# Building a graph's adjacency matrix on TensorE: edges by fixed chunks with sized windows, or by groups of ten targets

## The chip, the cores and the metric

The kernel runs on one core of a Trainium2 chip. The metric is the device time of one execution in microseconds; runs of the same kernel are compared by their median. Within a core, TensorE (PE) multiplies, VectorE (DVE) and ScalarE (ACT) do elementwise work, GpSimd (POOL) fills constants, and SyncE (SP) issues most of the transfers. Each engine works through its own instructions in order; semaphores tie them together.

## The reference

A graph has 1250 nodes with 512 features and 20,000 edges `src -> dst`, with the edges **sorted by dst**. Two graph layers follow each other, with a layer norm before and a residual after each. Cut to what matters here:

```
h  = relu(layernorm(x))
# layer 0
xn   = batchnorm(h)
agg  = segment_sum(xn[src], dst) / max(deg, 1)
conv = relu(agg @ W_conv + b_conv)
attn = kernel attention over the first 256 nodes (h @ Wq, h @ Wk, h @ Wv, random features, @ Wo)
x    = x + batchnorm(conv + attn + h)
# layer 1
h  = relu(layernorm(x))
z  = (1 + eps) * h + segment_sum(h[src], dst)
x  = x + h + relu(batchnorm(relu(batchnorm(z @ W1 + b1)) @ W2 + b2))
```

Both segment sums use the same edges. The kernel therefore builds a dense adjacency matrix of counts once (`adj`: 1250 sources in ten tiles of 128 rows, by 1250 targets), and both sums become products with it.

## The kernel before

**Two stages matter here.** `tile_gnn` (L1416) loads the edges and prepares keys: this is the prologue. It then loads the number `bad` into a register of every engine and branches: `sorted_graph` if the edges fit the plan, `any_graph`, a slow general arm, if they don't. At the start of `sorted_graph` the adjacency is built, with the attention's projections, the layer norms of the other nodes and the key features laid between its steps.

**How an adjacency is counted.** Take a set of edges, one edge in each of 125 partitions. Two one-hot matrices are made by VectorE with `is_equal` (`onehots`, L207): `op` marks the row of the source within its tile (128 columns), `ok` marks the pair of source tile and target within a window (10 tiles times the window's width). The matmul of `op` and `ok` then adds one for each edge in the right cell, in PSUM (`count`, L227). VectorE writes the one-hots of two chunks interleaved (the last index `i` of 2), which makes runs of 16-bit values.

**Fixed chunks, windows by position.** The 20,000 edges are 160 chunks of 125 in order. As the edges are sorted, chunk c has targets near a known place, and `width(c)` and `window(c)` (L54, L58) say at building time which targets it may touch: 24 wide at the ends, 38 in the middle. The prologue checks that each edge lies in its window. PSUM blocks hold 50 targets (`TB`), and a window that crosses a block's edge is cut by `pieces` (L63), so that 160 chunks make 266 matmuls of 10 to 380 columns. A batch is 8 chunks: 20 batches, one `op` of 1024 and one `ok` of 1920 to 3040 elements each. When a block has got its last chunk, ACT copies it to `adj` (L240). There are two `op`/`ok` buffers and two PSUM blocks.

**What lies between the batches.** `beside` (L319) is a generator: each `next(rest)` after a batch puts in one step of the attention. In order: `first_nodes` (L252: layer norm and transposes of the first 256 nodes, kept in `ed.x0`), five steps of `features` for the keys (L272, with Wk), eight pairs of scores and values (L294, L363, with Wv), then the queries (L272, with Wq, which takes Wk's place in SBUF when the keys are done), the batch norm's statistics (L351), the exponentials of the keys (L402). `node()` puts in the layer norm of one more tile of 128 nodes (L107 to L116, transposes L246). A list scheduler orders the instructions of an engine, except those marked `order(...)`, which keep the order of the code; the whole prologue is so marked.

**The prologue.** Two transfers bring `dst` and `src` as 80 partitions of two chunks each; two more bring the first 256 rows of x. VectorE subtracts the middle of the window, takes the largest distance (L1481) for `bad`, and splits the source into row and tile (L1492, L1494). PE transposes the keys (L1513), so that edges come to lie in partitions, and ACT writes them as `prow` and `kcol` (L1514). ACT also sums the first rows of x, and their squares, for the layer norm (L1503). PE runs multiplications of zeros (`keep_up`) to stay warm.

**The SP queue** after the branch: Wk, proj, eight tiles of x, Wv, eleven small vectors, W_conv; later Wq, eps, Wo.

After the build come the first products with W_conv (`product`, L442), the attention's second half, and the rest of both layers.

Of the kernel before, what the change touches and what calls it, by code (L numbers as in the profile page):

```python
# [14 lines left out]
I32 = mybir.dt.int32  # L15
AF = mybir.ActivationFunctionType
# [20 lines left out]
S = 128  # L37
# [3 lines left out]
CE = 125  # L41
CH = E // CE
NG2 = CH // 2


WIDTHS = [(4, 24), (12, 30), (20, 34), (NG2, 38)]
WMIN, WMAX = WIDTHS[0][1], WIDTHS[-1][1]
TB = 50
BQ = 4
# [3 lines left out]

def width(c):  # L54
    return next(w for m, w in WIDTHS if min(c // 2, NG2 - 1 - c // 2) < m)


def window(c):  # L58

    return min(max((CE * c + 62) // 16 - width(c) // 2, 0), N - WMIN)  # L60


def pieces(c):  # L63

    w, n = window(c), width(c)
    assert w + n <= N and (n == WMIN or 0 < w < N - n)
    return [(b, max(w - b * TB, 0), min(w + n - b * TB, TB), max(b * TB - w, 0))
            for b in range(w // TB, (w + n - 1) // TB + 1)]
# [12 lines left out]
def sorted_graph(ctx: ExitStack, tc: tile.TileContext, ed, x, n1g, n1b, n2g, n2b, wconv, bconv,  # L81
# [7 lines left out]
    ident, iota2, prow, kcol, epsc = ed.ident, ed.iota2, ed.prow, ed.kcol, ed.epsc  # L89
    order = tc.keep_in_program_order  # L90

    def weight(w, name, pool, tag):
        k, n = w.shape[0] // 128, w.shape[1]
        t = pool.tile([128, k, n], F32, name=name, tag=tag)
        nc.sync.dma_start(t, w.rearrange("(k p) n -> p k n", p=128))
        return t
# [77 lines left out]
    wkt = weight(wk, "k", ap2, "w")  # L174
# [5 lines left out]
    wvt = weight(wv, "v", ap2, "w")  # L180
# [23 lines left out]

    prow, kcol = (t.rearrange("p g k -> p (g k)").rearrange("p (b q i) -> p b q i", q=BQ, i=2) for t in (prow, kcol))

    def onehots(bt, parts=(BQ,)):  # L207
        w = NJ * width(2 * BQ * bt)
        o = (WMAX - w // NJ) // 2
        op = ohp.tile([CE, BQ, S, 2], F16, name="op")  # L210
        ok = ohp.tile([CE, BQ, NJ * WMAX, 2], F16, name="ok")
        q = 0
        for n in parts:
            qs = slice(q, q + n)
            for t, keys, c0, k in ((op, prow, 0, S), (ok, kcol, o, w)):
                i = nc.vector.tensor_tensor(t[:, qs, :k, :],  # L216
                                            iota2[:, c0:c0 + k, :].unsqueeze(1).to_broadcast([CE, n, k, 2]),
                                            keys[:, bt, qs].unsqueeze(2).to_broadcast([CE, n, k, 2]), ALU.is_equal)
                if len(parts) > 1:
                    order(i)  # L220
            q += n
        return op, ok

    acc = {}
    left = [sum(1 for c in range(CH) if any(b == t for t, _, _, _ in pieces(c))) for b in range(N // TB)]

    def count(bt, op, ok):  # L227
        for q in range(BQ):
            for i in range(2):
                c = (bt * BQ + q) * 2 + i  # L230
                okc = ok[:, q, :NJ * width(c), i].rearrange("p (j w) -> p j w", w=width(c))
                for b, lo, hi, w0 in pieces(c):
                    first = b not in acc
                    if first:
                        acc[b] = accp.tile([S, NJ, TB], F32, name="acc")
                    left[b] -= 1
                    nc.tensor.matmul(acc[b][:, :, lo:hi], op[:, q, :, i], okc[:, :, w0:w0 + hi - lo],  # L237
                                     start=first, stop=(left[b] == 0), skip_group_check=True)
                    if left[b] == 0:
                        nc.scalar.copy(adj[:, :, b * TB:(b + 1) * TB], acc.pop(b))  # L240
# [11 lines left out]
    def first_nodes():  # L252
        rs = tmp.tile([S, NT], F32, name="rs0")
        nb = tmp.tile([S, NT], F32, name="nb0")
        nc.scalar.activation(rs, ed.sq0, AF.Sqrt, bias=epsc, scale=1.0 / D)
        nc.vector.reciprocal(rs, rs)
        nc.vector.tensor_tensor(nb, ed.mean0, rs, ALU.mult)
        for j in range(NT):
            t = tmp.tile([S, D], F32, name="hn", tag="row")
            nc.scalar.activation(t, ed.x0[:, j, :], AF.Relu, bias=nb[:, j:j + 1], scale=rs[:, j:j + 1])  # L260
            transposed(j, t)
# [57 lines left out]
    def beside():  # L319
# [14 lines left out]
        keys = features(wkt, "k")  # L334
# [7 lines left out]
        wqt = weight(wq, "q", ap2, "w")  # L342
# [77 lines left out]
    nbt = CH // (2 * BQ)  # L420
    ahead = onehots(0, (1, 1, 2))
    next(rest)
    for bt in range(nbt):
        oh, ahead = ahead, onehots(bt + 1, (BQ,) if bt else (2, 2)) if bt + 1 < nbt else None
        count(bt, *oh)
        next(rest, None)
# [86 lines left out]
    wot = weight(wo, "o", ap2, "w")  # L513
# [451 lines left out]
def any_graph(ctx: ExitStack, tc: tile.TileContext, x, src, dst, n1g, n1b, n2g, n2b, wconv, bconv,  # L965
# [20 lines left out]
    def weight(w, name, pool, tag):  # L986
# [3 lines left out]
        return t  # L990

# [171 lines left out]
    def features(w, name):  # L1163
        wt = weight(w, name, ap1, "w")
# [50 lines left out]
    wt = weight(wv, "v", ap1, "w")  # L1215
# [54 lines left out]
    wt = weight(wo, "o", ap1, "w")  # L1270
# [34 lines left out]
    wct = weight(wconv, "wconv", cp, "wconv")  # L1305
# [110 lines left out]
def tile_gnn(ctx: ExitStack, tc: tile.TileContext, x, src, dst, *rest):  # L1416
# [6 lines left out]
    ed.iota2 = pre.tile([CE, NJ * WMAX, 2], F16, name="iota2")  # L1423
    ed.prow = pre.tile([CE, NG2, 2], F16, name="prow")
    ed.kcol = pre.tile([CE, NG2, 2], F16, name="kcol")
    ed.x0 = pre.tile([S, NT, D], F32, name="x0")
    ed.mean0 = pre.tile([S, NT], F32, name="mean0")
    ed.sq0 = pre.tile([S, NT], F32, name="sq0")
    ed.epsc = pre.tile([128, 1], F32, name="epsc")
    ed.zeros = pre.tile([128, 512], F16, name="zeros")  # L1430
    flag = pre.tile([1, 2], F32, name="flag")
    bad = pre.tile([1, 1], I32, name="bad")
    with tc.tile_pool(name="raw", bufs=1) as raw, tc.tile_pool(name="rawp", bufs=1, space=PSUM) as rawp:
        dt = raw.tile([NG2, 2, CE], I32, name="dt")
        nc.sync.dma_start(dt, dst.rearrange("(g k e) -> g k e", k=2, e=CE))
        sr = raw.tile([NG2, 2, CE], I32, name="sr")
        nc.sync.dma_start(sr, src.rearrange("(g k e) -> g k e", k=2, e=CE))
        for j in range(NT):
            nc.sync.dma_start(ed.x0[:, j, :], x[j * S:(j + 1) * S, :])

        win = raw.tile([NG2, 2], I32, name="win")
        order(nc.gpsimd.iota(win, pattern=[[CE, 2]], base=62, channel_multiplier=2 * CE))
        iota1 = raw.tile([CE, NJ * WMAX], F16, name="iota1")
        order(nc.gpsimd.iota(iota1, pattern=[[1, NJ * WMAX]], base=0, channel_multiplier=0,
                             allow_small_or_imprecise_dtypes=True))
        wide = raw.tile([NG2, 1], F32, name="wide")
        order(nc.gpsimd.memset(wide, float(WMAX)))
        for (m, w) in reversed(WIDTHS[:-1]):  # L1450
            for base, step in ((-m, 1), (NG2 - 1 - m, -1)):
                order(nc.gpsimd.affine_select(out=wide, in_=wide, pattern=[[0, 1]], compare_op=ALU.is_ge,
                                              fill=float(w), base=base, channel_multiplier=step))
        order(nc.gpsimd.memset(ed.ident, 0.0))
        make_identity(nc, ed.ident, nomemset=True)
        order(nc.vector.memset(ed.epsc, EPS))
# [51 lines left out]
        for n, (t, c, shift) in enumerate(((pf, ed.prow, zero), (rel, ed.kcol, lift))):  # L1508
            if n == 0:
                total(0, zero, AF.Identity, sum0)  # L1510
# [45 lines left out]
```

## Time and profile before

| what | us |
|---|---|
| median of 3 runs | 386.99 (386.86 to 387.9) |
| the profiled execution | 388.38 |
| its span in the profile | 386.5 |
| PE busy in the span | 371.8 (96%), 1801 matmuls |
| VectorE busy in the span | 252.7 (65%) |
| ACT busy in the span | 159.8 (41%) |
| counting matmuls (L237), busy | 33.7, 266 matmuls |
| one-hot compares (L216), busy | 46.0, 46 instructions |

The profile shows one execution. A group's line reads: source line, engine, operation, output and inputs by the program's names, shapes, count, then busy time and the mean of one in ns, then idle time of the engine before it. A matmul's duration includes the time it takes to run through the array, while the next has already started, so durations of neighbours overlap and their sum exceeds the time they take. "Chain" means the work that ended last, followed back from the end of a stretch, each step to what released it.

### The profile page before, as it was taken

What the parts mean: (1) busy time and instruction counts of PE and PEld (TensorE: products, weight loads), DVE (VectorE), ACT (ScalarE), POOL (GpSimd) and SP (SyncE); (2) the same over time, 40 slices, a digit from 0 to 9 for tenths busy, and PEclk for the clock granted to TensorE, in tenths of its full rate; (3) what the DMA queues carried; (4) which work ended last, traced back from release to release, by engine and by line L of the source; (5) the groups of instructions that cost most, each with busy time, mean ns of one, the idle gap of its engine ahead of it and who ended that gap; (6) DMA issues with size and microseconds to landing.
All of it is one profiled execution on the core that took longest, in us unless ns stands there. A gap on an engine that the chain in (4) does not pass through costs nothing.

```text
span 386.5 us, 4859 instructions
## 1 busy us (share of the span) xinstructions
PE 371.8 (96%) x1801; PEld 270.1 (70%) x1801; DVE 252.7 (65%) x566; ACT 159.8 (41%) x312; POOL 36.6 (9%) x58
## 2 busy tenths in 40 slices
PE   7899999999999999999999999999999999999972
PEld 3666556648556579999867888777777777777751
DVE  6997999887758823869688522154782688412783
ACT  6687634973566443011136702132553452121230
POOL 5000000000000000500000006740044000000000
PEclk9899999999999999999999999999999999999995
DMA  4933002000000067000000000060000000000045
GB/s 143 362 122 109 2 0 110 0 2 1 2 1 0 2 209 273 2 0 3 0 1 2 0 0 2 0 217 3 0 0 3 1 0 2 0 0 1 2 133 140
DMA packets 13296, 17.83 MB, mean 46 GB/s; under 512 B 1453, under 2 KB 6669, under 8 KB 13265
## 3 DMA queue, kind: packets, MB, share of 16 engines
q1 hardware_dynamic: 10704, 16.19, 12.8%
q10 hardware_dynamic: 2560, 1.25, 1.2%
q8 instruction: 16, 0.26, 0.3%
q14 instruction: 16, 0.12, 0.1%
HBM read 14.88 MB, written 2.56 MB: 45 GB/s over the span
## 4 chain that ended last, share of the span: by engine, by line
PE 89%; DVE 6%; ACT 2%; issue 1%; DMA 1%; DVEq 0%; ACTq 0%
PE mm L785 28%; PE mm L728 12%; PE mm L596 11%; PE hw L442 8%; PE acc L237 7%; PE mm L272 4%; PE sc L294 3%; PE mm L542 2%; PE mm L470 2%; PE mm L503 2%; PE mm L363 2%; PE mm L246 2%; DVE xs L915 1%; PE mm L722 1%; PE mm L493 1%; PE mm L442 1%
## 5 line engine op out<-in xcount | busy, mean ns | idle before, releaser
L800 ACT ACTIVATE kept<-mm,vT 128x313 f32<-128x313 f32 x36 | 18.5, 520 | 49.6 <-PE mm L785 48.5
L237 PE MATMUL acc<-ok,op 125*128 125x380 f16 (+28 forms) x266 | 33.7, 271 | 0.0
L442 PE MATMUL hw<-wconv,xn 128*128 128x512 f32 (+1 forms) x72 | 33.4, 604 | 0.0
L728 PE MATMUL mm<-hi,adj 128*128 128x512 f32 (+2 forms) x100 | 32.1, 398 | 0.5 <-DVE hi L676 0.4
L216 DVE TENSOR_TENSOR ok<-iota,kcol 125x3040 f16<-125x3040 f16 (+6 forms) x23 | 31.9, 1387 | 0.3 <-ACT kcol L1514 0.3
L237 PEld LDWEIGHTS <-op 125*128 125x128 f16 x266 | 21.8, 101 | 14.1 <-issue 6.3
L728 PE MATMUL mm<-lo,adj 128*128 128x512 f32 (+2 forms) x100 | 31.7, 394 | 0.0
L140 ACT ACTIVATE r<-mv,epsc 128x1 f32<-128x1 f32 x16 | 4.7, 292 | 51.6 <-DVE mv L139 51.6
L785 PE MATMUL mm<-hid,w 128*128 128x313 f32 x96 | 25.8, 427 | 0.0
L596 PE MATMUL mm<-adj,hi 128*128 128x416 f32 (+3 forms) x120 | 25.1, 355 | 0.0
L596 PE MATMUL mm<-adj,lo 128*128 128x416 f32 (+3 forms) x120 | 25.0, 354 | 0.0
L805 DVE TENSOR_TENSOR hid<-mm,kept 128x313 f32<-128x313 f32 x24 | 10.9, 477 | 20.4 <-ACT kept L800 16.9
L442 PEld LDWEIGHTS hw<-wconv,xn 128*128 128x128 f32 (+1 forms) x72 | 12.7, 187 | 14.9 <-issue 14.4
L785 PEld LDWEIGHTS mm<-hid,w 128*128 128x128 f32 x96 | 18.1, 190 | 6.9
L596 PEld LDWEIGHTS mm<-adj,hi 128*128 128x128 f32 x120 | 21.9, 189 | 1.1
L596 PEld LDWEIGHTS mm<-adj,lo 128*128 128x128 f32 x120 | 21.7, 189 | 1.1
L728 PEld LDWEIGHTS mm<-hi,adj 128*128 128x128 f32 (+2 forms) x100 | 18.4, 186 | 5.7 <-DVE hi L676 1.4
L719 DVE SCALAR_TENSOR_TENSOR z<-h,e,mm 128x512 f32<-128x512 f32 (+1 forms) x10 | 7.0, 744 | 23.4 <-PE mm L728 15.6
L728 PEld LDWEIGHTS mm<-lo,adj 128*128 128x128 f32 (+2 forms) x100 | 18.5, 185 | 4.6 <-DVE lo L669 0.2
L805 DVE TENSOR_TENSOR o<-mm,kept 128x313 f32<-128x313 f32 x12 | 5.7, 481 | 21.5 <-ACT kept L800 20.8
L216 DVE TENSOR_TENSOR op<-iota,prow 125x1024 f16<-125x1024 f16 (+2 forms) x23 | 14.1, 612 | 6.1 <-PE acc L237 5.4
L785 PE MATMUL mm<-tz,w 128*128 128x313 f32 x64 | 17.5, 426 | 0.0
(241 smaller groups left out, 718.4 us busy)
## 6 DMA issues: line engine op xcount, KB each, us to landing
w<-in_L_gnn_W_dram SPq DMA_DIRECT2D x2, 2048.0 KB
x<-in_x_dram SPq DMA_DIRECT2D x9, 256.0 KB
xs<-in_x_dram SPq DMA_DIRECT2D x9, 256.0 KB
k<-in_L_gnn_Wk_dram SPq DMA_DIRECT2D x1, 1024.0 KB
v<-in_L_gnn_Wv_dram SPq DMA_DIRECT2D x1, 1024.0 KB
wconv<-in_L_gnn_W_conv_dram SPq DMA_DIRECT2D x1, 1024.0 KB
q<-in_L_gnn_Wq_dram SPq DMA_DIRECT2D x1, 1024.0 KB
o<-in_L_gnn_Wo_dram SPq DMA_DIRECT2D x1, 1024.0 KB
```

The costliest lines, as they stand in the source:

```text
L216: i = nc.vector.tensor_tensor(t[:, qs, :k, :], iota2[:, c0:c0 + k, :].unsqueeze(1).to_broadcast([CE, n, k, 2]), keys[:, bt, qs].unsqueeze( ...
L237: nc.tensor.matmul(acc[b][:, :, lo:hi], op[:, q, :, i], okc[:, :, w0:w0 + hi - lo], start=first, stop=(left[b] == 0), skip_group_check=True)
L246: nc.tensor.transpose(ps[:, f, :n], t[:n, f * 128:(f + 1) * 128], ident[:n, :n])
L272: nc.tensor.matmul(ps, wt[:, k, b * 128:(b + 1) * 128], hT[:, k, :TOK], start=(k == 0), stop=(k == KD - 1))
L294: nc.tensor.matmul(ps[:, a, :M], tT[a * 64:a * 64 + 64, b, t * 128:(t + 1) * 128], projT[a * 64:a * 64 + 64, :], start=True, stop=True)
L363: nc.tensor.matmul(pv, hT[:, b, t * 128:(t + 1) * 128], wvt[:, b, :], start=(b == 0), stop=(b == KD - 1))
L442: nc.tensor.matmul(ps[:n], xn[:, f, :n], wct[:, f, :], start=(f == 0), stop=(f == KD - 1))
L596: nc.tensor.matmul(ps, part[:k, j, fs], adj[:k, j, c], start=(part is hi and j == 0), stop=(part is lo and j == NJ - 1))
L728: nc.tensor.matmul(ps[:n], adj[:k, j, t * S:t * S + n], part[:k, j, :], start=(part is hi and j == 0), stop=(part is lo and j == NJ - 1))
L785: order(nc.tensor.matmul(banks[i], left[:, k, m * 128:(m + 1) * 128], right[:, k, i * NH:(i + 1) * NH], start=(p in (1, 2, 5) and k == 0), ...
L800: nc.scalar.activation(t[:, c, :], self.A[c], AF.Identity, bias=self.part(i, 0, c)[1], scale=1.0)
L805: order(nc.vector.tensor_tensor(self.part(i, j, c)[0], self.B[c], t[:, c, :], ALU.add))
```

## The change

The edges are no longer cut at fixed places but at the targets. 1250 targets make 125 groups of ten, and the chip itself finds where each group's edges begin:

- The edges are loaded with overlap: partition p holds the 400 edges from 160 p on (124 partitions), as ten possible starts, 16 edges apart, each followed by at least 256 edges. `kd` is dst, `ks` is src. The transfers go over the SP and the ACT queue.
- `sample` is every sixteenth dst; `less` compares it with the first target of every group (126 x 10), and ten matmuls with ones sum over partitions: `cnt` is for each group the number of whole sixteens of edges ahead of it, in every partition.
- `pick` is a one-hot of `begin` (that number) over the possible starts. 60 matmuls (dst, row of the source, tile of the source times 1280; two halves of 128 edges; ten starts) with `pick` bring the 256 edges of a group's slot into 2 x 128 partitions: `keys`.
- `prow` is the row of the source; `kcol` is tile x 1280 + dst - first target of the group, as int16. Edges of the slot that belong to other groups find no equal in the comparison.
- `bad` is set if the edges aren't sorted, or if a group ends outside its slot.
- In the build a batch is five groups, that is one PSUM block of 50 targets: 25 batches of ten matmuls, each with 128 edges and 100 columns. `op` has 1280 elements, `ok` 1000, and `ok` compares int16 with int16. ACT's copy of a block to `adj` stays.
- `next(rest)` is called after three of four batches.
- The first 256 rows of x are normalized in place in the prologue, one tile's statistics on ACT, the other's on VectorE; `first_nodes` only transposes.
- Wk is loaded in the prologue, into a tile of its own (`ed.wk`), in which Wq follows it. Wv and Wo share one buffer. The general arm uses `ed.wk` as well.

```diff
@@ sorted_graph
-    wkt = weight(wk, "k", ap2, "w")
...
-    wvt = weight(wv, "v", ap2, "w")
+    wvt = weight(wv, "v", ap2, "w", bufs=1)
...
+    def onehots(bt, parts=(BG,)):
+        op = ohp.tile([128, BG, S, 2], F16, name="op")
+        ok = ohp.tile([128, BG, NJ * TG, 2], F16, name="ok")
         q = 0
         for n in parts:
             qs = slice(q, q + n)
...
+            for t, keys, iota in ((op, prow, ed.iop), (ok, kcol, ed.iok)):
+                shape = [128, n, iota.shape[1], 2]
+                i = nc.vector.tensor_tensor(t[:, qs], iota.unsqueeze(1).to_broadcast(shape),
+                                            keys[:, bt, qs].unsqueeze(2).to_broadcast(shape), ALU.is_equal)
...
     def count(bt, op, ok):
-        for q in range(BQ):
+        acc = accp.tile([S, NJ, TB], F32, name="acc")
+        for q in range(BG):
             for i in range(2):
...
+                nc.tensor.matmul(acc[:, :, q * TG:(q + 1) * TG], op[:, q, :, i],
+                                 ok[:, q, :, i].rearrange("p (j t) -> p j t", t=TG),
+                                 start=(q == 0 and i == 0), stop=(q == BG - 1 and i == 1), skip_group_check=True)
+        nc.scalar.copy(adj[:, :, bt * TB:(bt + 1) * TB], acc)
...
     def first_nodes():
...
+            transposed(j, ed.x0[:, j, :])
...
-    ahead = onehots(0, (1, 1, 2))
+    ahead = onehots(0, (2, 3))
...
-        next(rest, None)
+        if bt % 4 != 3:
+            next(rest, None)
@@ tile_gnn
+        edges(nc.sync, kd, dst, 0, 96, 0, SPAN)
+        edges(nc.scalar, kd, dst, 96, KP, 0, few)
+        order(nc.vector.memset(kd[96:, few:], 0))
+        order(nc.vector.memset(ks[96:, few:], 0))
+        edges(nc.scalar, kd, dst, 96, KP - 1, few, SPAN)
+        edges(nc.sync, ks, src, 0, 96, 0, SPAN)
+        edges(nc.sync, ks, src, 96, KP, 0, few)
+        edges(nc.sync, ks, src, 96, KP - 1, few, SPAN)
...
+        order(nc.sync.dma_start(ed.wk, wk.rearrange("(k p) n -> p k n", p=128)))
...
+        order(nc.vector.tensor_copy(sample, kd[:, STEP - 1:STEP * RB:STEP]))
...
+        order(nc.vector.tensor_tensor(less, sample.unsqueeze(1).to_broadcast([KP, NGR + 1, RB]), first, ALU.is_lt))
...
+        for b in range(RB):
+            order(nc.tensor.matmul(cnt, more if b == RB - 1 else ones, less[:, :, b],
+                                   start=(b == 0), stop=(b == RB - 1)))
...
+        order(nc.scalar.copy(kd16, kd))
...
+        order(nc.vector.tensor_tensor(out, kd16[:, :few - 1], kd16[:, 1:few], ALU.is_gt))
+        order(nc.vector.tensor_reduce(wrong, out, AX.X, ALU.max))
...
+        keep_up(4)
...
+        order(nc.vector.tensor_scalar(pi, ks, S - 1, None, op0=ALU.bitwise_and))
+        order(nc.scalar.copy(pk, pi))
...
+        order(nc.vector.tensor_scalar(begin, cnt[:KP, :NGR], float(LAST), None, op0=ALU.min))
...
+        order(nc.vector.tensor_tensor(pick, begin.unsqueeze(1).to_broadcast([KP, RB, NGR]), start, ALU.is_equal))
+        order(nc.vector.tensor_scalar(ji, ks, 7, None, op0=ALU.logical_shift_right))
+        order(nc.scalar.activation(jk, ji, AF.Copy, scale=float(JK)))
...
+        for i, (t, kind) in enumerate(parts):
+            for h in range(2):
+                for b in range(RB):
+                    c = STEP * b + 128 * h
+                    order(nc.tensor.matmul(keys[:, kind, h, :], t[:, c:c + 128], pick[:, b, :],
...
+        order(nc.vector.scalar_tensor_tensor(bad, most, SLOT // STEP - 0.5, wps, op0=ALU.is_ge, op1=ALU.max))
...
+        for func, bias, scale, i in ((AF.Identity, zero, -1.0 / D, 0), (AF.Square, acc[:, 0:1], 1.0, 1)):
+            order(nc.scalar.activation(junk, ed.x0[:, 0, :], func, bias=bias, scale=scale, accum_out=acc[:, i:i + 1]))
...
+            order(nc.scalar.activation(ed.x0[:, j, :], ed.x0[:, j, :], AF.Relu, bias=nb[:, j:j + 1], scale=r))
+        order(nc.scalar.copy(ed.prow, keys[:, 1].rearrange("p h g -> p g h")))
+        order(nc.vector.tensor_tensor(ed.kcol, keys[:, 0].rearrange("p h g -> p g h"),
+                                      lead.unsqueeze(2).to_broadcast([128, NGR, 2]), ALU.subtract))
```

## The prediction, made before the result was known

> **What bounds the kernel now.** I read three views: the busy times of long stretches, the chain of waits inside the second stretch, and VectorE in order of time. All times are in microseconds from the start of the profiled span (386.5; that execution took 388.38 in all, 1.4 more than the median of the runs, 386.99; I carry a difference over to the median as it stands).
>
> ```profile
> 0.00:10.75 10.75, 7.50 (x27) 3.48 (x27) 7.02 (x27) 7.13 (x17) 4.95 (x29) 1.00 0.55 166
> 10.75:79.90 69.15, 68.92 (x438) 44.53 (x439) 63.06 (x117) 45.94 (x98) 0.76 (x7) 0.98 0.28 93
> 79.90:386.50 306.60, 295.37 (x1338) 222.11 (x1336) 182.66 (x423) 106.69 (x199) 30.89 (x22) 0.98 0.10 31
> ```
>
> The columns are length, then busy time of PE, PEld, DVE, ACT, POOL, the granted clock, DMA. The change touches the first two stretches only: the prologue up to the first transposes (10.75) and the build of the adjacency, which ends where the first product with W_conv starts (79.9). From there PE runs on for 306.6 with nothing of the change in it, so that part moves as a block.
>
> ```profile
> by line: PE acc L237 41.7%; PE mm L272 20.5%; PE mm L363 9.4%; PE sc L294 9.1%; PE mm L246 8.4%; PE mm L275 4.6%; PE mm L280 1.5%; ACT hn L116 1.2%; DVE op L216 1.0%; PE mm L286 0.6%; PE mm L324 0.6%; PE mm L388 0.5%; PE mm L344 0.3%; issue
> ```
>
> This is the chain inside 10.75 to 79.9: the counting matmuls (L237) hold 28.8 of the 69.15, other PE work 38.4, everything else 1.9. But PE is not alone. In order of time VectorE reads:
>
> ```profile
> 49.81 0.67 DVE L216 TENSOR_TENSOR op<-iota,prow 125x1024 f16<-125x1024 f16 x1
> 50.41 1.73 DVE L216 TENSOR_TENSOR ok<-iota,kcol 125x3040 f16<-125x3040 f16 x1
> 52.06 0.68 DVE L360 TENSOR_REDUCE kmx<-sc 128x2 f32<-128x512 f32 x1
> 52.66 0.58 DVE L351 BATCH_NORM_STATS2 gst<-hT 128x6 f32<-128x416 f32 x1
> 53.16 0.67 DVE L216 TENSOR_TENSOR op<-iota,prow 125x1024 f16<-125x1024 f16 x1
> ```
>
> There is no idle time between them: one batch of edges costs VectorE 3.35 here, and 2.25 of it are the two one-hot compares. Over the stretch VectorE is 91% busy (63.06 of 69.15). So the build has two engines at the bound, and a gain needs both to shrink.
>
> **PE in the build.** Removed: the 255 counting matmuls after 10.75, 52,800 columns by the kernel's windows. Added: 25 batches of 10 matmuls of 100 columns. Their price is in the trace, since the windows cut some matmuls to that width:
>
> ```profile
> L237 PE MATMUL acc<-ok,op 125*128 125x380 f16 x20 | 6.2, 333 | 0.0
> ...
> L237 PE MATMUL acc<-ok,op 125*128 125x100 f16 x6 | 1.4, 230 | 0.0
> ```
>
> The means are latencies (some 0.18 each before the columns count). What a stream pays is the distance of starts, which I took from the start times of neighbours: 0.168 to 0.170 behind most matmuls of 380 columns, 0.071 to 0.074 at 130, 0.051 to 0.057 for four of the five at 100, 0.026 to 0.031 for the narrowest. That is about 0.42 ns a column, plus little. 250 x 0.055 = 13.8. The old ones by the same rate are 22.0, while the chain has 28.8: 6.8 are ends of runs, where PE turns to other work. There are again as many turns; I leave half of it, 3.4, as they overlap better with less behind them. New sum 17.2, a saving of **11.6** on PE; with all of the 6.8 left it is 8.2.
>
> Here a rule speaks against the change. The Trainium skill ("TensorE: Matmul & The Clock Gate", section Back-to-back issue gap) says that a real stream of weight load and matmul pairs takes about 81 ns each at 128 columns, as both set the pace. Every one of these matmuls has its own weights. By the rule the 250 take 20.3 instead of 13.8, and the saving falls to about 5. The trace has weight loads of 0.10, but they start down to 0.015 apart; and 100 columns did take 0.055. No long run of narrow ones is in it, though, so I take the row and keep the rule's value for the range.
>
> **VectorE in the build.** One `op` now has 1280 elements, one `ok` 1000, 25 times each. From start to start the old ones take 0.61 (1024) and 1.65 (3040), with 0.52 ns for each more element: 0.74 and 0.59, so 1.33 a batch and **33.3** in all. The 39 compares after 10.75 occupy 38.1 by the same count; the other work of VectorE in the stretch is 63.1 - 38.1 = 25.0 and stays. The open price is that `ok` now compares int16 with int16, which no row shows. Bounds: the f16 row (0.59), and the f32 compare-like sum
>
> ```profile
> L452 DVE TENSOR_TENSOR dsum<-dsum,adj 128x1250 fp32r<-128x1250 f32 x3 | 4.4, 1456 | 0.0
> ```
>
> which makes 1.10 of 1000 elements; 25 x 0.51 = 12.7 more. The Trainium skill ("VectorE: DVE Perf Modes", What auto-detection actually checks) asks for 16-bit types and unit steps in every tensor, not for floats; int16 meets that, so I take 0.59 and keep 1.10 for a rival.
>
> **The prologue.** Before, VectorE starts its first one-hots at 5.95 and PE its first transposes at 10.75, behind ACT's four passes over the first rows of x (from 6.39, 0.83 each with its accumulator read). The chain up to there starts with
>
> ```profile
> 0.74 1.97 DMA dt<-in_dst_dram
> ...
> 2.80 0.43 DVE rel L1477
> ...
> 3.25 0.41 DVE off L1481
> ...
> 4.26 0.41 ACT pf L1493
> ...
> 4.71 1.36 PE keyps L1513 x4
> ```
>
> After, step by step. The edges come in six pieces over two queues, 0.3 MB instead of 0.16; the first needed ones land at about 2.9. ACT issues two of these (some 0.4 each on its queue) ahead of its 1.28 table load, which still ends by 3.2, before its first cast. `sample` 0.17, `less` (1260 f16, 0.73): 3.8. Ten count matmuls of 126 columns while PE is still slow (the warming matmuls of 512 columns start 0.427 apart up to about 8): 0.105 each, 5.1. VectorE meanwhile does `out`, `wrong`, `pi` (0.4, 0.45, 0.36), so `begin` ends at 5.5. `pick` has 1250 f16 in runs of 125: 0.74 by the f16 rows, 1.45 by the f32 sum of the same size; I take the former: 6.3. PE has four warming matmuls in between (1.7, to 7.0), then 60 key matmuls of 125 columns: ten slow at 0.105, fifty at 0.062, to about 11.2 (13.3 if all are slow). `ji` and ACT's `jk` are done at 7.2, under that. ACT then goes over x in place: two passes (1.7), two roots (0.55), VectorE's small steps (0.35), two Relu (1.5), to 11.3, `prow` to 11.8; `kcol` on VectorE (250 from PSUM, 0.42) to 11.8. So the first one-hots start near **11.9**, 6 later than before, and hT follows at 12.5 to 13.2, where it was 12.4 to 13.0. `bad` is known at about 7.2 against 4.9, so SP passes the branch, and the loads of x1, Wv, the vectors and W_conv behind it start 2.3 later; but Wk (1 MB, 3 at the 345 GB/s of 8 to 20) has gone ahead of the branch, into a time in which the queue is empty after x, so x1 is complete at about the same time, near 16. Wk is there before 9, its first use at 13. PE's queue order puts nothing else behind these. POOL's iotas (two of 1250, about 1.3 each by 0.45 for 380) are done by 5, ahead of `pick`. Without that cover each microsecond would go straight into the start.
>
> **The sum.** PE could be through the build at 12.2 + 38.4 - 1.6 (transposes done) + 17.2 + 1.9 = 68.1. VectorE starts at 11.9 and needs 33.3 + 25.0 = 58.3: 70.2 if never idle, 76.0 at the 91% of before. Half of the removed stalls on `acc` buffers (5.4 in all, before `op`) should go, as PE frees them faster: 95%, **73.3**, against 79.9. ACT has 45.9 of work in this stretch and the exponentials of the keys at its end, 12 to 13 behind `kb`; what is left of them falls under the first two products (3.6 each) and the reads of `kf` after these. So the block of 306.6 starts 6.6 earlier, and I round to 7: 386.99 - 7 = **380.0**.
>
> **Rivals.**
> 1. VectorE fills no better and the prologue is some 2 longer (`pick` at one element a cycle, keys all slow): 76.0 + 2 to 3, the build ends at 78 to 79 and 386 is measured. For it: the prologue is a chain over four engines, each with little slack. Against: it needs both.
> 2. Slower: the int16 compare runs at 1.10. VectorE then has 71.0 from 11.9: 82.9 when never idle, 85 at 97%; +3 to +5, so 391. It decides from 0.25 more a compare on. For it: no int16 row; against: the rule above.
> 3. Weight loads set the pace of narrow matmuls (0.081 to 0.1): PE 12.2 + 36.8 + 25 x 0.9 + 5 = 76.5 at 0.09, keys 1.5 later: 384.5.
> 4. The edges don't satisfy the new test and the other arm runs. Ten targets have 160 edges on average and a slot takes 240 at least, over six standard deviations of a random draw: 1%, and far slower.
>
> **Chances.** Forecast (376.5 to 384) 0.60, rival 1 0.12, rival 2 0.16, rival 3 0.10, the rest 0.02. Runs of this kernel differ by 0.3% (1.2), which I count as no change. Faster: the forecast, most of 3, a little of 1: 0.70; same 0.09; slower 0.21, as the prologue could be worse than each row of it. The range runs from 375.5 to 390.
>
> **What would show it.** The `ok` compare at 0.66 and not 1.2; starts of counting matmuls 0.055 apart; first one-hots at 12; PE at the first W_conv product at 73; VectorE over 93% busy in between, with kmx and the statistics between compares 1.3 long. It is wrong if PE waits for `op` or `ok` in the rounds with keys' projections, or if the loads of x1 land after 17 and the layer norms wait.

## The result and the profile after

The changed kernel took **784.69** (783.14 to 785.38, four runs) against 387.44 (386.86 to 388.18) for the kernel before: a ratio of 2.025, interval 2.019 to 2.030. All times are in microseconds. The forecast was 380.0.

A change of 7 in a build of 69 cannot cost 397, so the first question is not which step became slow but which program ran. The page of the changed kernel, busy times and then the costliest groups (line, engine, operation, tiles, count; busy time and mean in ns; idle time before):

```profile
span 781.4 us, 7923 instructions
...
PE 621.5 (80%) x3129; PEld 378.5 (48%) x3129; DVE 360.0 (46%) x769; ACT 116.3 (15%) x223; POOL 100.4 (13%) x82
...
L1090 PE MATMUL acc<-oh 125*125 125x128 f16 x1600 | 98.8, 221 | 18.1 <-DVE adj L1094 17.7
...
L1306 PE MATMUL mm<-adj,h 125*128 125x417 f32 (+1 forms) x240 | 88.7, 529 | 17.7 <-ACT h L977 17.6
L1086 DVE TENSOR_SCALAR oh<-iot,ends 125x1250 f16<-125x1250 f16 x160 | 87.2, 545 | 4.1 <-PE acc L1090 3.4
```

PE carries out 3129 matmuls where it had 1801, and 1600 of them count edges at L1090. That line belongs to `any_graph` (from L935 of the changed kernel), the general arm. The compares (L201) and counting matmuls (L212) of `sorted_graph` do not occur in the trace at all. SyncE in order of time shows the turn:

```profile
3.32 0.43 SPq L1426 DMA_DIRECT2D wk<-in_L_gnn_Wq_dram  x1
...
11.62 0.32 SPq L953 DMA_DIRECT2D g1r<-in_L_gnn_norm_g_dram  x1
...
13.26 0.28 SPq L1024 DMA_DIRECT2D src_i<-in_src_dram  x1
```

L953 and L1024 are the general arm's first loads; at 13.26 it loads `src` once more, from the start. So the prologue ran to its end, `bad` was set, and every engine took the other branch. Rival 4 of the prediction happened, the one that had been given 1%.

The first row shows a second thing. The early load of "Wk" brings Wq: the code takes `rest[6]`, and `rest` is n1g, n1b, n2g, n2b, W_conv, b_conv, Wq, Wk. The general arm loads its weights again itself:

```profile
wk<-in_L_gnn_Wq_dram SPq DMA_DIRECT2D x2, 1024.0 KB
wk<-in_L_gnn_Wk_dram SPq DMA_DIRECT2D x1, 1024.0 KB
```

**Why `bad` was set** can be worked out from the edges and three lines of the prologue. Call 16 edges that follow each other a sixteen; there are 1250. `sample` takes the last dst of each, ten in each of 124 partitions, which covers sixteens 0 to 1239. The rest is stood for by a weight: `more`, the ones of the last of the ten count matmuls, has a fill value `E // STEP - KP * RB` = 10 in partition 123, so sixteen 1239 counts ten times.

In these edges target 1240 first occurs at edge 19,856, that is 16 x 1241. Sixteen 1239 lies ahead of it and counts ten: `cnt` for target 1240 becomes 1239 + 10 = 1249, where 1241 whole sixteens lie ahead. The group of targets 1230 to 1239 begins at 1229, so it seems to end 20 sixteens on, and `bad` is set from 15.5. The true distance is 12. Every other group's is at most 15, and the fullest group has 185 edges, so the slots do hold the edges: the test rejects a graph that the plan fits. For the mark behind the last target, 1250, the weight serves: it gives 1249, and the last group, from 1234 on, passes with 15. It is wrong for any earlier target that begins behind sixteen 1239.

### The profile page after: what moved, and what is told of

The parts are those of the page before. It is cut to its first block, busy times and chain, and to the rows that moved or that the text cites. A ratio compares the mean times of both kernels' runs of the same rounds, so it can differ in the third digit from the quotient of the medians.

```text
span 781.4 us, 7923 instructions
## 1 busy us (share of the span) xinstructions
PE 621.5 (80%) x3129; PEld 378.5 (48%) x3129; DVE 360.0 (46%) x769; ACT 116.3 (15%) x223; POOL 100.4 (13%) x82
## 4 chain that ended last, share of the span: by engine, by line
issue 33%; PE 21%; DVE 10%; POOL 1%; ACT 1%; DVEq 0%; POOLq 0%
PE mm L1306 11%; PE mm L1316 4%; DVE deg L1292 3%; PE mm L1259 2%; DVE h L975 1%; PE stat L992 1%; DVE xs L1385 1%; PE stat L984 1%; POOL o L1384 1%; DVE h L1323 1%; DVE xn L1284 1%; DVE xn L1285 1%; DVE ln_st L971 1%; PE mm L1296 1%; PE mm L1234 1%
## 5 line engine op out<-in xcount | busy, mean ns | idle before, releaser
L1090 PE MATMUL acc<-oh 125*125 125x128 f16 x1600 | 98.8, 221 | 18.1 <-DVE adj L1094 17.7
L1090 PEld LDWEIGHTS <-oh 125*125 125x125 f16 x1600 | 98.2, 138 | 26.8 <-issue 23.6
L1306 PE MATMUL mm<-adj,h 125*128 125x417 f32 (+1 forms) x240 | 88.7, 529 | 17.7 <-ACT h L977 17.6
L1086 DVE TENSOR_SCALAR oh<-iot,ends 125x1250 f16<-125x1250 f16 x160 | 87.2, 545 | 4.1 <-PE acc L1090 3.4
L1306 PE MATMUL mm<-adj,xn 125*128 125x417 f32 (+1 forms) x240 | 84.6, 514 | 0.0
L1306 PEld LDWEIGHTS mm<-adj,h 125*128 125x128 f32 x240 | 45.9, 195 | 60.7 <-issue 36.0
L1361 PE MATMUL mm<-zT,w 128*128 128x417 f32 (+1 forms) x192 | 69.8, 526 | 0.0
L1378 PE MATMUL mm<-w,hid 128*125 128x512 f32 x160 | 68.8, 592 | 0.0
L1306 PEld LDWEIGHTS mm<-adj,xn 125*128 125x128 f32 x240 | 45.8, 191 | 39.3 <-issue 39.3
L1087 DVE TENSOR_SCALAR oh<-iot,ends 125x128 f16<-125x128 f16 x160 | 39.8, 249 | 0.0
```

Of the source, the lines that this page charges most:

```text
L1086: nc.vector.tensor_scalar(oh[:, :N], iot, s[:, k:k + 1], None, op0=ALU.is_equal)
L1087: nc.vector.tensor_scalar(oh[:, N:], iot[:, :W], d[:, k:k + 1], None, op0=ALU.is_equal)
L1090: nc.tensor.matmul(acc[:, j * W:(j + 1) * W], oh[:, j * P:(j + 1) * P], oh[:, N:], start=(k == 0 and j % 4 == 0), stop=(k == NC - 1), skip ...
L1306: nc.tensor.matmul(ps, t[:, j, f * 128:(f + 1) * 128], adj[:, j, n0:n0 + n], start=(j == 0), stop=(j == NB - 1))
L1361: nc.tensor.matmul(ps, w1t[:, k, m * 128:(m + 1) * 128], zT[:, k, n0:n0 + n], start=(k == 0), stop=(k == KD - 1))
L1378: nc.tensor.matmul(ps, hid[:, m, j * P:(j + 1) * P], w2t[:, m, :], start=(m == 0), stop=(m == KH - 1))
```

## The experiments

The theory for the first three kernels was this weight; the rival was that something else about the edges (their order, or the other part of `bad`) sends them to the general arm.

**1. The weight alone.** One number:

```diff
-                                      fill=float(E // STEP - KP * RB), base=KP - 2, channel_multiplier=-1))
+                                      fill=1.0, base=KP - 2, channel_multiplier=-1))
```

> The changed kernel with one number changed: the weight of the last sampled sixteen in the count, 1 instead of 10. Wq's weights still stand where the keys' should, so the keys are computed with Wq instead of Wk; the work is the same. Theory A (this weight alone makes the test say no: it counts 1249 sixteens ahead of target 1240 where 1241 are, which leaves 20 for the group before, over the 15.5 allowed): the sorted arm runs, 380 to 396 us. Theory B (the sortedness check or another part of the test says no): still about 785 us.

Measured: 384.16 (one run), span 382.4. The sorted arm ran. With weight 1 the mark behind the last target counts 1240 instead of 1249, so the last group's end is tested less strictly; no instruction is added or taken away.

**2. The weight, and Wk in place of Wq.** Besides the line above:

```diff
-        wk = rest[6]
+        wk = rest[7]
```

> As the run before, and the prologue loads Wk (entry 7 of the arguments) instead of Wq (entry 6). Theory A as in my prediction, with the prologue as the trace of the changed kernel has it (keys ready at 17.5 instead of 11.8, so 5.7 later): build ends at 79, 386 us, ratio about 1.0. Theory A2 (int16 compares take 1.10 instead of 0.59): 396 us. Theory A3 (narrow matmuls at 0.08 or more): 388 to 390 us. Theory B: 785 us.

Measured: 383.79 (383.50 to 384.16); ratio to before 0.991 (0.989 to 0.993).

**3. Wk alone**, the weight left at 10.

> The changed kernel with only the prologue's load corrected to Wk. Theory A (the count's weight alone decides the branch): no change, 785 us, the general arm runs. Rival (the wrong weights have to do with the time): below 400 us.

Measured: 785.48 (one run). So the weight decides alone, and which matrix is loaded early has no part in it. This settles the 397.

What remained was the forecast's own subject: what the change is worth when its arm runs. From here kernel 2 stands for it, 3.4 faster than before instead of 7. Its three stages, in the columns of the prediction (length, busy PE, PEld, DVE, ACT, POOL, clock, DMA):

```profile
0.00:18.60 18.60, 12.00 (x85) 7.42 (x86) 8.60 (x24) 7.07 (x14) 11.74 (x28) 0.82 0.58 190
18.60:76.30 57.70, 54.62 (x437) 35.48 (x435) 56.21 (x132) 44.53 (x97) 0.96 (x9) 1.00 0.24 85
76.30:382.40 306.10, 293.57 (x1336) 221.12 (x1333) 182.06 (x423) 106.76 (x199) 30.87 (x22) 0.99 0.10 31
```

The build is shorter than forecast and VectorE is 97% busy in it (56.21 of 57.70). But it starts at 18.6 and not at 11.9. The chain of waits of kernel 2, from its start to `bad`, says who made the prologue long:

```profile
0.87 4.09 POOL first L1429
...
5.21 0.85 POOL more L1438
6.06 1.28 POOL start L1429
7.34 0.36 POOL lead L1429
7.70 1.49 POOL iop L1429
9.19 0.68 POOL iok L1429
...
10.60 0.04 POOL one L1481
10.64 0.04 POOL zero L1521
...
10.69 0.20 PE wps L1482 x2
...
10.92 0.15 DVE bad L1513
```

GpSimd is on the path from the beginning. The two constants that it writes last, 0.1 each, hold back the small matmul `wps` (L1482), and all of PE's work behind that in its order: four warming matmuls and sixty key matmuls.

**4. The constants first.** `one` and `zero` are set before the ramps; theory A: the wait for them is on the path to the first one-hots; B: something else ends last anyway.

```diff
+        one = raw.tile([KP, 1], F32, name="one")
+        order(nc.gpsimd.memset(one, 1.0))
+        zero = raw.tile([S, 1], F32, name="zero")
+        order(nc.gpsimd.memset(zero, 0.0))
...
-        one = raw.tile([KP, 1], F32, name="one")
-        order(nc.gpsimd.memset(one, 1.0))
...
-        zero = raw.tile([S, 1], F32, name="zero")
-        order(nc.gpsimd.memset(zero, 0.0))
```

> As e2, with GpSimd's two small fills (the ones for the sortedness sum, the zero bias) ahead of its ramps. In the trace of the changed kernel PE waits 2.34 for the second of them before the sum, the warming matmuls and all 60 key matmuls. If that wait is on the path: keys 1.5 to 2.3 earlier, the same off the whole time against e2. If pick (done at 8.4) or the build takes it back: less than 1.

Measured: 381.43 (380.82 to 382.05), ratio 0.986 (0.984 to 0.987), 2.4 less than kernel 2 on the same chip. The key matmuls start at 10.19 instead of 12.50, so theory A holds: two memsets at the wrong place in a queue cost some 2.4. A part may be PE's pace and not the wait. In kernel 2's profile the granted clock was 0.50 from 10 to 14 (0.82 over the whole stage, as above) and the key matmuls took 4.75 in all; in kernel 4's it was 1.00 and they took 3.93. So the first one-hots came even 2.86 earlier in these two executions (15.73 instead of 18.59). The one execution of kernel 2 with kernel 4's mean clock (0.988) took 383.50, 2.1 more than kernel 4.

**5. `less` by start, and a short ramp.** GpSimd's first ramp has 126 rows of ten equal values and takes 4.13; and the count matmuls read `less` at every tenth element.

```diff
-        first = raw.tile([KP, NGR + 1, RB], F16, name="first")
-        iota(first, [[TG, NGR + 1], [0, RB]])
+        first = raw.tile([KP, NGR + 1], F16, name="first")
+        iota(first, [[TG, NGR + 1]])
...
-        less = raw.tile([KP, NGR + 1, RB], F16, name="less")
-        order(nc.vector.tensor_tensor(less, sample.unsqueeze(1).to_broadcast([KP, NGR + 1, RB]), first, ALU.is_lt))
+        less = raw.tile([KP, RB, NGR + 1], F16, name="less")
+        order(nc.vector.tensor_tensor(less, sample.unsqueeze(2).to_broadcast([KP, RB, NGR + 1]),
+                                      first.unsqueeze(1).to_broadcast([KP, RB, NGR + 1]), ALU.is_lt))
...
-            order(nc.tensor.matmul(cnt, more if b == RB - 1 else ones, less[:, :, b],
+            order(nc.tensor.matmul(cnt, more if b == RB - 1 else ones, less[:, b, :],
```

> As e4, with the comparison `less` laid out by starts (each of the ten count matmuls reads 126 values in a row, not every tenth) and GpSimd's first ramp 126 values instead of 1260. In e4 the ramp lasts 4.13 and the cast `sample`, ten values, ends only with it (1.59); the ten count matmuls start 0.22 apart. Theory A (VectorE's cast is held by GpSimd's ramp, and the matmuls by the stride of what they read): sample 0.2 to 0.6, count matmuls 0.105 apart, less 1.4 instead of 0.82; keys some 2 earlier, ratio to e4 0.994 to 0.996. Theory B (the ten casts and the matmuls are slow by themselves, being cold): 0.5 slower than e4.

Measured: 380.92 (380.47 to 381.01) on another chip. Its ratio to before is 0.983 (0.981 to 0.984), where kernel 4 had 0.986, so it is some 1.1 faster; the keys start at 9.21, 1.0 earlier, where 2 had been expected. Nine count matmuls now take 1.10 from first start to last end instead of 2.20, and the ramp 0.26. But `less`, with `sample` repeated along its inner axis, went from 0.82 to 1.47, and `sample` stayed slow. VectorE in order of time in kernel 5 (start, duration, engine, line, operation, tiles, shapes, idle before):

```profile
3.45 1.22 DVE L1468 CAST sample<-kd 124x10 f16<-124x10 int32 x1 [2.02 <-DMA kd<-in_dst_dram]
4.77 1.47 DVE L1470 TENSOR_TENSOR less<-sample,first 124x1260 f16<-124x1260 f16 x1
```

and GpSimd in the same kernel:

```profile
3.10 1.53 POOL L1429 IOTA iop<- 128x256 f16 x1
```

A cast of ten values takes 1.22 and ends at 4.67, when the ramp that happens to run, `iop`, has just ended (4.63). In kernel 2 it ended at 4.99, the ramp `first` at 4.96; in kernel 4 at 5.06, the ramp at 5.03. The cast reads nothing of `iop`, so it was held by GpSimd itself, not by what GpSimd wrote.

**6, 7, 8: banks, warming, an exact count.** Kernel 6 puts the keys of dst and src into two PSUM tiles:

```diff
-        keys = rawp.tile([128, 2, 2, NGR], F32, name="keys")
+        keys = [rawp.tile([128, 2, NGR], F32, name=f"keys{k}") for k in range(2)]
```

> As e5, with the two kinds of keys in two PSUM tiles, so that ACT's copy of the source rows need not wait for all 60 key matmuls and VectorE's kcol not for ACT. In e4 kcol starts 0.8 behind the last key matmul, and PE's first transposes, whose PSUM comes from the same place, behind kcol. Theory A: 0.4 to 0.8 faster than e5. Theory B (VectorE is late by then for another reason, or the transposes wait for ACT): no difference.

Kernel 7 is kernel 6 with `keep_up(1)` in place of `keep_up(4)` ahead of the key matmuls:

> As e6, with one warming matmul instead of four ahead of the keys. Four take 1.9 of PE's queue, and the keys are behind them. Theory A (pick is done earlier than they end): up to 1 faster. Theory B (pick comes at the same time, or PE stays slow for the keys without them: 0.105 against 0.062 each): no gain, or 1 to 2 slower.

Kernel 8 is kernel 7 with the sample made complete: 125 partitions, so that the formula's weight is 0 and no sixteen stands for others (the last sixteen of all lies ahead of no target, so that it needs no weight).

```diff
-KP = E // (STEP * RB) - 1
+KP = E // (STEP * RB)
```

Its loads are cut anew, and the rows that reach past the end are filled up.

> As e7, with 125 partitions of edges instead of 124, so that every sixteen of edges is counted and none stands for ten; the test is then exact for the last groups. Two short transfers more. No more than 0.5 slower than e7.

Measured, on one chip with kernel 5: 379.97 (379.19 to 380.80), 381.02 (380.44 to 381.40) and 380.86 (380.33 to 381.97). Two tiles seem to bring 0.95. The trace shows where: in kernel 5 `kcol` starts 1.0 behind the end of the last key matmul (12.80), released by ACT's copy `prow`; in kernel 6 it starts 0.1 behind it (14.27), released by PE. Kernel 5, then kernel 6:

```profile
13.77 0.42 DVE L1538 TENSOR_TENSOR kcol<-keys,lead 128x250 int16<-128x250 f32 x1 [1.64 <-ACT prow L1537]
```

```profile
14.38 0.42 DVE L1538 TENSOR_TENSOR kcol<-keys,lead 128x250 int16<-128x250 f32 x1 [2.26 <-PE keys L1507]
```

All the same `kcol` came 0.6 later in this execution of kernel 6, its longest (380.80), as the first forty key matmuls took 2.31 and 1.80 instead of 1.30 each twenty. Why, with the same four warming matmuls, no run here shows. Leaving out three warming matmuls costs 1.05. In kernel 7 PE's order is:

```profile
8.80 2.26 PE L1507 MATMUL keys<-pick,kd 124*128 124x125 f16 x20 [0.64 <-DVE pick L1496]
10.85 2.31 PE L1507 MATMUL keys<-pick,pk 124*128 124x125 f16 x20
12.95 1.88 PE L1507 MATMUL keys<-pick,jk 124*128 124x125 f16 x20
```

Twenty of these take 1.30 when PE is fast (the last twenty of kernel 6). PE started on them 0.43 earlier than in kernel 6, but was slow for longer, so that they ended at 14.83 instead of 14.27. The granted clock is 1.00 from 8 to 14 in both profiles, so that column does not show this kind of slowness. Kernel 8 shows that a count without a stand-in costs nothing that can be measured.

**9. GpSimd waits for `sample`.** Kernel 8 with the four warming matmuls back, and a small copy on GpSimd that reads `sample`, put ahead of the ramps that nobody needs yet:

```diff
+        gate = raw.tile([KP, RB], F16, name="gate")
+        order(nc.gpsimd.tensor_copy(gate, sample))
         start = raw.tile([KP, RB, NGR], F16, name="start")
...
-        keep_up(1)
+        keep_up(4)
```

> As e8, with four warming matmuls again and with GpSimd held until VectorE's cast `sample` is done (a copy of sample on GpSimd ahead of its other ramps). In five traces the cast of ten values ended 0.02 to 0.04 behind a ramp on GpSimd, whichever ran, and took 0.55 to 1.7. Theory A (VectorE's cast can't finish while GpSimd runs a ramp): the cast takes 0.2 and everything up to the keys comes 0.8 to 1 earlier; about 379.5 to 380. Theory B (the cast waits for something of its own, a late piece of the transfer): it takes over 1 again, and no difference.

Measured: **379.87** (379.19 to 380.02), ratio 0.981 (0.979 to 0.982), 1.0 less than kernel 8, which ran on another chip (ratio 0.984). VectorE and then GpSimd:

```profile
3.67 0.18 DVE L1462 CAST sample<-kd 125x10 f16<-125x10 int32 x1 [1.83 <-DMA kd<-in_dst_dram]
```

```profile
3.91 0.20 POOL L1464 COPY gate<-sample 125x10 f16<-125x10 f16 x1 [2.16 <-DVE sample L1462]
4.06 1.32 POOL L1432 IOTA start<- 125x1250 f16 x1
```

With GpSimd at rest the cast takes 0.18, where the prediction had 0.17: this settles what held it. It shows no gain in time, though. `less` ends 0.87 earlier than in kernel 8 (5.43 against 6.30), but `pick` only 0.15 (8.40 against 8.55), as `out`, `wrong` and `pi` stand between them in VectorE's order, and the key matmuls start at nearly the same time (8.54 against 8.60). They end 1.1 earlier (12.52 against 13.66), with four warming matmuls and a granted clock of 1.00 from 8 to 12, where kernel 8's profile has about 0.6 and 0.5. Kernel 6, with four warming matmuls and no gate, has the same ratio to before (0.980). So most of the 1.0 is likely PE's pace. This version has the whole change, its arm runs, and it is faster than both kernels.

**10. Wk behind the branch.** Kernel 9 with the load of Wk put back where it was before:

```diff
+    nc.sync.dma_start(ed.wk, wk.rearrange("(k p) n -> p k n", p=128))
...
-        wk = rest[7]
-        order(nc.sync.dma_start(ed.wk, wk.rearrange("(k p) n -> p k n", p=128)))
```

> As e9, with Wk's transfer behind the branch again, first of its queue, as it was before the change. Theory A (the early load matters because the branch is later now): Wk lands 5 behind the branch and the eight tiles of x 3 later; the first keys' step and the layer norms wait, 2 to 4 slower than e9. Theory B (the first batches cover it): no difference.

Measured: 383.12 (382.91 to 383.43), 3.25 more than kernel 9. The first one-hots start at 13.97, 0.43 later than in kernel 9 (13.54); the rest comes behind that. SyncE in kernel 10:

```profile
10.89 0.39 SPq L162 DMA_DIRECT2D wk<-in_L_gnn_Wk_dram  x1
...
12.40 5.55 SPq L159 DMA_DIRECT2D x<-in_x_dram  x8
```

Wk's megabyte stands ahead of the eight loads of x1, which are issued until 17.95; in kernel 9 they are issued from 11.41 to 15.22. The first projections with Wk start at 20.14 instead of 16.92 and take 3.57 instead of 1.96, at a granted clock of 0.66 (20 to 25; kernel 9 had 1.00). The first product with W_conv starts at 73.41 instead of 68.91. So the early load pays; how much of the 3.25 is the clock is not shown.

**11. Fewer compares.** Kernel 9 with 11 of the 25 `op` compares left out (these batches count with the `op` of the batch before):

```diff
+        half = bt > 1 and bt % 2
+        op = last_op[0] if half else ohp.tile([128, BG, S, 2], F16, name="op")
+        last_op[0] = op
...
-            for t, keys, iota in ((op, prow, ed.iop), (ok, kcol, ed.iok)):
+            for t, keys, iota in ((op, prow, ed.iop), (ok, kcol, ed.iok))[1 if half else 0:]:
```

> As e9, but eleven of the 25 `op` comparisons are left out (an odd batch from the third on uses the op of the batch before it, so the adjacency it counts is another one). VectorE has 8.0 less to do in the build. Theory A (VectorE bounds the build, PE is 3 behind it): 2.5 to 4 faster than e9, PE nearly without gaps then. Theory B (PE bounds it): under 1. Theory C (VectorE alone, with PE far behind): 7 to 8.

Measured: 376.80 (376.53 to 377.02), 3.07 less than kernel 9, for 8.0 less work on VectorE. So VectorE's work limits the time, and something else stands close behind: VectorE's `ok` now waits 3.8 in all for PE's counting. In the trace the first product with W_conv comes only 0.8 earlier (68.13 against 68.91), but with all batches counted, and the rest of the gain lies behind it. That VectorE alone bounds the build is not shown. It is 98% busy in kernel 9's build, yet the chain of waits there (13.54 to 68.9) lies on PE for 26 of 55, on VectorE for 12.5 and on ACT for 10.7.

## Why the prediction was wrong, point by point

**The step that failed is rival 4's price.** It read: "Ten targets have 160 edges on average and a slot takes 240 at least, over six standard deviations of a random draw: 1%". That sentence tests whether a group fits its slot, and this is true: the fullest has 185. It does not test what the kernel tests, which is `cnt` for the next group less `begin`, and `cnt` contains the weight of `more`. The count matmul with `more` was in view (it was priced, with nine others, at 0.105), its fill value was not worked out. Put into numbers for the group next to last, the test gives 20 against a limit of 15.5. By the same arithmetic on 1000 random draws of the same kind, 513 fail with 124 partitions and weight 10, and none with 125 and weight 0. So the chance to give was about a half, before any profile is read; with the reference's own edges it could have been made a certainty.

The arm's price could not have come from the profile of before, where not one instruction of it ran. "Far slower" was all that could be said.

**The forecast itself, for its own arm**, can be held against kernel 2, and against kernel 9:

| step | predicted | kernel 2 | kernel 9 |
|---|---|---|---|
| `sample`, `less` done | 3.8 | 5.91 | 5.43 |
| `pick` done | 6.3 | 9.64 | 8.40 |
| key matmuls start | 7.0 | 12.50 | 8.54 |
| key matmuls done | 11.2 | 17.25 | 12.52 |
| first one-hots | 11.9 | 18.59 | 13.54 |
| first W_conv product | 73.3 | 73.96 | 68.91 |
| one batch of counting inside the products | 0 | 0.46 | 0.46 |
| from there to the end of the span, without that batch | 306.6 | 308.0 | 308.1 |
| median time | 380.0 | 383.79 | 379.87 |

- **Prologue: 6.7 too short** against kernel 2. The misses are: `less` done 2.1 late, 1.5 of it because `sample`, held by GpSimd, took 1.67 instead of 0.17; the count matmuls 0.22 apart instead of 0.105, as they read every tenth element (1.1); and the wait of `wps` for `one`, with the warming matmuls behind it (2.2). In the order of PE's queue these make 5.4 of the 5.5 by which the keys start late; the key matmuls (0.55, at the low granted clock named at kernel 4) and the step from them to the one-hots (0.6) add the rest. On the chain of waits, though, all of the late start is GpSimd's queue: with `less` on time PE would still have waited for GpSimd until 10.69. The cast and the stride count only once that wait is gone, as in kernel 5. The prediction said of GpSimd that its ramps take 1.3 each and are done by 5. They had been priced by element; `first` took 4.13 for 1260 values in rows of ten, and GpSimd was busy until 10.7. The prediction even warned that each microsecond without that cover goes straight into the start, and did not follow POOL's queue to its end.
- **Build: 5.6 too long.** From the first one-hots to the first product it takes 55.4 in kernel 2, and 0.46 for the batch that comes later; 61.4 were predicted. VectorE's compares came as summed. In the order of time of kernel 2:

```profile
49.12 0.81 DVE L201 TENSOR_TENSOR op<-iop,prow 128x1280 f16<-128x1280 f16 x1
49.84 0.67 DVE L201 TENSOR_TENSOR ok<-iok,kcol 128x1000 f16<-128x1000 int16 x1
50.43 0.82 DVE L201 TENSOR_TENSOR op<-iop,prow 128x1280 f16<-128x1280 f16 x1
51.17 0.68 DVE L329 TENSOR_REDUCE kmx<-sc 128x2 f32<-128x512 f32 x1
51.77 0.67 DVE L201 TENSOR_TENSOR ok<-iok,kcol 128x1000 f16<-128x1000 int16 x1
```

  From start to start `op` takes 0.72 to 0.74 and `ok` 0.59, against 0.74 and 0.59. What was too large is the rest: VectorE is busy for 54.5 up to the first product (58.3 were summed), partly because its last small steps come behind that point; and it fills 98% of that stretch, not 95%.
- **The block behind the build: 1.2 longer than before.** The first W_conv product of before starts at 79.74 and not at 79.9, so its block is 306.8; kernel 2's is 308.0. All of the difference arises before the first product with the adjacency: this comes 67.6 behind the first W_conv product without the late batch, and came 66.2 behind it before. The prediction had moved the block as it was; what made it longer is open.
- **The int16 compare (rival 2) runs at the price of f16**, as the rule on 16-bit types from the Trainium skill ("VectorE: DVE Perf Modes", section What auto-detection actually checks) had it. The group in kernel 2 has a mean of 666 ns; 1.2 would have meant rival 2:

```profile
L201 DVE TENSOR_TENSOR op<-iop,prow 128x1280 f16<-128x1280 f16 x23 | 18.6, 808 | 0.5 <-PE acc L212 0.4
...
L201 DVE TENSOR_TENSOR ok<-iok,kcol 128x1000 f16<-128x1000 int16 x23 | 15.3, 666 | 0.0
```

- **The counting matmuls (rival 3)** show the row's price and not the rule's. In kernel 2 ten of them start at 50.75 and the next work on PE at 51.21:

```profile
50.75 0.62 PE L212 MATMUL acc<-ok,op 128*128 128x100 f16 x10
51.21 1.09 PE L332 MATMUL mm<-v,hT 128*128 128x512 f32 x2
```

  That is 0.046 each, where the row gave 0.055 and the rule, for 128 columns, 0.081, and every one has its own weights. The key matmuls of kernel 4, with 125 columns, start 0.057 apart (twenty of them from 11.68 to 12.82). The twenty-five batches are 11.5 instead of 13.8. What this gave in time no run shows. By the prediction's own terms, too, rival 3 is 385 and not 384.5: 76.5 and keys 1.5 later make 78.0, 1.9 less than 79.9.
- **x1 landed late**, at about 21 in kernel 2 (the chain has its transfer from 16.31 for 4.83) where 16 was predicted, since `bad` came at 11.06 and not at 7.2. VectorE filled 98% of the build all the same. The prediction had made this a sign that it is wrong; it was one for the prologue. That Wk has to go ahead of the branch was right: kernel 10, without it, took 3.25 more.
- **Rival 1** said that a longer prologue would leave 386. The prologue was longer by three times what it assumed, and the shorter build paid for most of it.

That kernel 9 measures almost what was forecast doesn't confirm the steps. In the spans its errors are 1.6 (first one-hots), -5.6 (build) and +1.5 (the block behind it), -2.5 in all; 2.1 of that is the choice of execution, as the profiled one of before lay 1.4 above its median and that of kernel 9 lies 0.7 below. And its prologue has edits that the change doesn't have.

## What to carry to other kernels

Where a program chooses between two arms by a test on the data, work the test through on the data, constant by constant, before any duration is summed: here one fill value decided some 400 and all steps of the timing together 7. A test can also refuse what the plan could do, so "the data fit" is not the same statement as "the test passes". In a prologue, follow the queue of the engine that only fills constants to its very end, and put first what others wait for: two memsets of 0.1 at its end cost some 2.4. And a shorter step gives only what the next wait leaves of it: the gate took 0.8 off a cast, and at `pick` 0.15 of it was left.

## What the runs showed of the hardware

- **A VectorE cast waits for a running GpSimd ramp.** The same cast of ten int32 values took 0.55, 1.67, 1.59, 1.22 and 1.02 in the changed kernel and in kernels 2, 4, 5 and 8, each time ending within 0.04 of the end of the ramp that ran, and 0.18 with GpSimd at rest (kernels 9, 10 and 11). A `tensor_scalar` of 400 int32 took 0.88 beside ramps (kernel 2) and 0.36 without (kernel 5). A compare of two f16 tensors, `pick`, took 0.82 beside two ramps (kernel 2). GpSimd's selection `more`, which reads a tensor, was the one held there: 0.85 beside VectorE's `less` in kernel 4, 0.29 with VectorE idle in kernel 5. The Trainium skill ("SBUF — State Buffer", section Who interferes with whom) has the rule: casts and `tensor_scalar` may use a port pair that VectorE shares with GpSimd, which is held for a whole instruction, and a compare of two SBUF tensors contends only with GpSimd instructions that read. The prediction had not drawn on it; the rows here agree with it.
- **A ramp's time follows its rows more than its values.** 1250 values in 10 rows took 1.32; 256 values in 128 rows of two 1.53; 1260 values in 126 rows of ten 2.68 (the changed kernel) and 4.13 (kernels 2 and 4); 126 values in one row 0.26. Why that one ramp took two different times is open.
- **A strided moving operand slowed the count matmuls**: nine of 126 columns took 2.20 with a step of ten f16 elements (kernel 4) and 1.10 when the columns lay together (kernel 5), both while PE was slow (nine that lay together took 0.67 in kernel 8). The counting matmuls of the build, with a step of two elements, show no such price (0.046 for 100 columns).
